# Scores from stacked high and low parts of q and k, in one-pass products, with q and k made two attentions ahead

## The chip, the core and the metric

The kernel runs on one core of a Trainium2 chip. The metric is the device time of one execution in microseconds (us), from the first to the last instruction. The profile shows one execution: each engine's instructions with start and duration, the waits between engines, and the packets of the DMA engines. TensorE does matrix products, VectorE (DVE in the profile) and ScalarE (ACT) elementwise work, GpSimd (POOL) elementwise work and some DMA issues, and SyncE (SP) only issues DMAs here. Each engine works through its own instructions in the order in which they were written.

## What is computed

Sixteen independent sequences of 256 tokens with 256 features pass through three attentions and an MLP. All data is fp32, with 16 heads of 16 features. The reference, cut down:

```python
q_norm = rmsnorm(query, g_q); c_norm = rmsnorm(context, g_c)          # layer 0
out = softmax(Q K^T * scale, masked keys) V  @ Wo
x = rmsnorm(query + out, g_out)
h = ln(x); q, k, v = h @ wq + bq, ...                                  # layer 1
x = x + attn(rope(q * scale), rope(k), v, causal=True) @ wo + bo
h = ln(x); q = h @ wq + bq; k, v = y @ wk + bk, y @ wv + bv            # layer 2
x = x + attn(rope(q * scale), rope(k), v, causal=False) @ wo + bo
x = x + gelu(ln(x) @ fc1 + b1) @ fc2 + b2
```

Layer 0 is a cross attention of x to the context y, layer 1 a causal self attention, layer 2 again a cross attention to y. So there are 48 attentions of 16 heads each.

## The kernel before

**Order of the work.** The 48 attentions run one after the other in an order written by hand (`ORDER`, one digit for each attention, the digit being its layer): layer 0 of several sequences first, then layers 1 and 2 mixed in, so that an attention's input is ready some attentions earlier. After them come the MLPs of pairs of sequences. All instructions are placed by hand under a manual schedule: the loop over `i` (line 1020) emits, for each block `n` of attention `i`, the scores of this block, the values of the block before, and then pieces of the work of attentions around it. What is emitted first on an engine is done first there, and a wait of one instruction holds up all that stand behind it on the same engine, SP's queue of DMAs included. I call the time from one attention's first scores to the next one's a slot.

**One attention.** Features lie on partitions in two chunks `t` of 128, that is 8 heads each; tokens lie on the free axis. `by_feature` (line 345) makes q and k this way, `by_token` (line 356) makes v and the output projection. In both, a product is split into four of 32 columns that write to different partitions and run side by side in the array.

**Scores.** A non-causal attention has four blocks, one for each pair of chunk `t` and key chunk `kc` (128 keys); a causal one has three. In `scores` (line 553) the array is cut the other way, in four groups of 32 rows. Each group holds two heads of 16 features, so the kernel masks q: `qm` holds q twice, once with the even heads zeroed and once with the odd ones (`parity`). One fp32 product of 32 rows of k with both masked q's, 512 columns, gives the scores of the two heads. The result goes to two PSUM tiles `S`, which ACT empties by the exponential into `pt`. `psS` has two buffers, so the next block's scores wait for both exponentials. In causal attentions GpSimd zeroes what lies above the diagonal (line 584). `values` (line 589) multiplies the exponentials with v, one product for each head, and keeps a column of ones in v for the sums.

**q and k.** `q` (line 481) and `k` (line 520) are emitted one attention ahead, in slot `i` for attention `i+1`. For layer 0, q is scaled by the row's root mean square and masked in two DVE instructions straight out of PSUM, and k is copied by ACT. For layers 1 and 2, `rotated` (line 463) adds the bias on ACT, then DVE shuffles a copy by half a head and multiplies both by cosine and sine tables; DVE adds them, and for q masks the sum twice (one mask sometimes on ACT, `second_mask`).

**After the values.** `take` (line 619) copies the values out of PSUM (ACT for the first chunk, DVE for the second, in `end`) and writes them to a DRAM tile `hop`; `end` then reads the sums back with one DMA and the heads with two (`oT`). `invert` (line 637) takes the reciprocals on DVE, writes them to `inv_hop` and reads them back broadcast (`inv`). `divide` multiplies, `project` applies the output weights and adds the residual, `finish` norms layer 0's result. All these DMAs stand in SP's queue.

**Turning.** The input of layers 1 and 2 has to be turned so that features lie on partitions. For most attentions DVE transposes blocks of 32 (`pieces_out`), SP writes them to a DRAM tile `turn_hop` and four DMAs bring them back (`pieces_in`), in a slot chosen by `turned_ahead`. The others are turned by TensorE (`turn`). For layer 0 the input is loaded already turned, and the factor for q goes through a small DRAM tile (`send`, two DMAs, and `receive`).

**Buffers.** Tiles of the pool `work` have two buffers unless said otherwise; PSUM has three banks for dense products (`psD`), two pairs for scores (`psS`) and one for values (`psA`).

## Time and profile before

| | us |
|---|---|
| median of 3 runs (927.35 to 927.95) | 927.66 |
| span of the profiled execution | 927.3 |
| from the first scores of attention 0 to those of attention 2 (10.1 to 41.9) | 31.8 |
| attentions 2 to 47, 46 slots (41.9 to 721.2) | 679.3 |
| MLP and rest (721.2 to the end) | 206.1 |
| TensorE busy | 913.6 |
| DVE busy | 689.0 |
| ACT busy | 531.0 |
| GpSimd busy | 348.7 |

A line of the profile that describes a group names the line of the kernel, the engine, the operation, the tiles written and read, shapes and count; then the busy time in us, the mean duration in ns, and the idle time of the engine just ahead of these instructions, with what ended it. An fp32 product appears as two records. Records of products that run side by side overlap, so their busy time is less than count times mean. Lines that describe the order of time begin with the start in us and the time that the piece took. A line marked SPq is a DMA issue: its time is that of issuing, and the transfer follows.

### The profile page before, as it was taken

The page shows a single profiled execution, that of the slowest core. Times are in us where ns is not written, and L with a number is a line of the kernel's source. Part 1 is how long each engine was busy: PE and PEld are TensorE (multiplying, and loading weights), DVE is VectorE, ACT ScalarE, POOL GpSimd, SP SyncE. Part 2 cuts the span into 40 slices and gives each one's busy share as a digit, 9 for nine tenths or more (in the row PEclk, how much of TensorE's full clock was granted, in tenths as well). Part 3 has the DMA queues.
Part 4 walks back from the last instruction along what each step waited for, and adds up shares of the span by engine and source line. Part 5 has one row for each costly group of instructions (what it writes and reads, how often), then busy time and mean ns, then how long its engine had stood idle before and what let it go on. Part 6 is the DMA issues. An engine that isn't in the chain of part 4 may idle for free.

```text
span 927.3 us, 29346 instructions
## 1 busy us (share of the span) xinstructions
PE 913.6 (99%) x12226; PEld 535.3 (58%) x12226; DVE 689.0 (74%) x1501; ACT 531.0 (57%) x744; POOL 348.7 (38%) x558
## 2 busy tenths in 40 slices
PE   8999999999999999999999999999999999999997
PEld 4444445445454555455445454455444799999997
DVE  4458678896879787968977778987877597777663
ACT  3666546665666665657656666666666633444440
POOL 4224655446363564633554432453233041111100
PEclk9999999999999999999999999999999999999999
DMA  9443554355243243442444433333222111122201
GB/s 292 159 116 108 156 151 146 123 153 145 87 144 115 92 151 107 133 126 83 136 138 131 128 107 104 92 98 108 85 82 67 54 38 47 55 69 69 70 24 48
DMA packets 112193, 100.52 MB, mean 108 GB/s; under 512 B 24299, under 2 KB 104051, under 8 KB 112051
## 3 DMA queue, kind: packets, MB, share of 16 engines
q1 hardware_dynamic: 106962, 83.59, 28.8%
q0 software_dynamic: 4400, 14.42, 5.3%
q8 instruction: 98, 1.61, 0.8%
q10 hardware_dynamic: 688, 0.54, 0.2%
q14 instruction: 45, 0.36, 0.1%
HBM read 59.70 MB, written 38.82 MB: 106 GB/s over the span
## 4 chain that ended last, share of the span: by engine, by line
PE 89%; DVE 6%; DMA 2%; issue 1%; SPq 1%; ACT 0%; POOL 0%; DVEq 0%
PE S L566 18%; PE A L605 17%; PE d L352 16%; PE d L364 15%; PE upX L788 6%; PE A L886 5%; PE downZ L886 3%; PE upZ L788 3%; PE d L886 2%; PE d L788 2%; DVE a L476 1%; DVE u L476 1%; PE d L286 1%; DVE u L472 1%; PE downX L886 1%
## 5 line engine op out<-in xcount | busy, mean ns | idle before, releaser
L577 ACT ACTIVATE pt<-S 128x1024 f32<-128x1024 f32 x224 | 217.3, 1022 | 134.0 <-PE S L566 133.9
L566 PE MATMUL S<-qm,kT 32*128 32x512 f32 (+1 forms) x1536 | 202.9, 601 | 4.7 <-DVE kT L525 4.5
L605 PE MATMUL A<-pt,va 128*32 128x256 f32 (+1 forms) x3072 | 189.6, 368 | 0.0
L605 PEld LDWEIGHTS A<-pt,va 128*32 128x32 f32 x3072 | 80.2, 109 | 154.3 <-issue 95.5
L577 ACT ACTIVATE pt<-S,sy 128x1024 f32<-128x1024 f32 x128 | 135.6, 1111 | 50.6 <-PE S L566 50.3
L584 POOL TENSOR_SCALAR_AFFINE_SELECT pt<-pt 128x512 f32<-128x512 f32 x128 | 86.3, 688 | 141.1 <-ACT pt L577 140.7
L566 PEld LDWEIGHTS S<-qm,kT 32*128 32x128 f32 x1536 | 62.4, 183 | 76.1 <-issue 42.1
L468 ACT ACTIVATE a<-d,qk_bias 128x256 f32<-128x256 f32 x128 | 53.7, 470 | 52.1 <-PE d L352 36.1
L340 POOL TENSOR_TENSOR cur<-cur,bias 128x512 f32<-128x512 f32 x48 | 69.7, 1458 | 31.6 <-DVE xn L271 31.3
L352 PE MATMUL d<-hT,sa 128*32 128x256 f32 x1024 | 61.1, 379 | 0.2 <-DMA hT<-turn_hop 0.2
L246 POOL TENSOR_SCALAR r_ln<-bmv 128x2 f32<-128x2 f32 x48 | 13.1, 272 | 125.8 <-DVE bmv L265 124.3
L476 DVE TENSOR_TENSOR u<-u,turn 128x512 f32<-128x512 f32 x64 | 57.3, 895 | 0.0
L810 ACT COPY g<-upX 128x512 f32<-128x512 f32 x28 | 15.0, 589 | 72.4 <-issue 67.5
L476 DVE TENSOR_TENSOR a<-a,turn 128x512 f32<-128x512 f32 x64 | 52.5, 821 | 2.2
L622 DVE COPY av<-A 128x512 f32<-128x512 f32 x47 | 32.0, 681 | 22.3 <-PE A L605 21.7
L472 DVE STREAM_SHUFFLE u<-a 128x512 f32<-128x512 f32 x64 | 47.4, 741 | 0.0
L826 ACT ACTIVATE g<-g,fb 128x256 f32<-128x256 f32 x96 | 41.0, 499 | 11.1 <-DVE g L815 11.1
L352 PEld LDWEIGHTS d<-hT,sa 128*32 128x32 f32 x1024 | 33.4, 110 | 22.2 <-issue 0.6
L656 DVE TENSOR_TENSOR oT<-oT,inv 128x512 f32<-128x512 f32 x48 | 38.3, 799 | 10.2 <-issue 6.3
L246 POOL TENSOR_SCALAR r_o<-ms_o 128x2 f32<-128x2 f32 x16 | 4.7, 293 | 105.7 <-DVE sq L254 98.5
L271 DVE TENSOR_SCALAR xn<-cur,bmv,r_ln 128x256 f32<-128x256 f32 x96 | 41.6, 483 | 0.8 <-POOL r_ln L247 0.8
L665 DVE TENSOR_TENSOR cur<-d,cur 128x512 f32<-128x512 f32 x32 | 21.6, 674 | 26.3 <-PE d L364 26.1
(158 smaller groups left out, 1612.5 us busy)
## 6 DMA issues: line engine op xcount, KB each, us to landing
hop<-av SPq DMA_DIRECT2D x96, 256.0 KB
oT<-hop SPq DMA_DIRECT2D x96, 128.0 KB
inv<-inv_hop SPq DMA_DIRECT2D x96, 128.0 KB
turn_hop<-turn SPq DMA_DIRECT2D x33, 256.0 KB
hT<-turn_hop SPq DMA_DIRECT2D x132, 64.0 KB
out<-res SPq DMA_DIRECT2D x15, 256.0 KB
cur<-in_x POOLq DMA_DIRECT2D x11, 256.0 KB, 3.4
y<-in_y POOLq DMA_DIRECT2D x11, 256.0 KB, 4.2
```

What stands on the lines that cost most here:

```text
L340: nc.gpsimd.tensor_tensor(t, t, bias_sb[:, row : row + D].unsqueeze(1).to_broadcast([P, NC, D]), ALU.add)
L352: nc.tensor.matmul(o, lhsT=w[:, k, at + t * P + j : at + t * P + j + 32], rhs=tokens, start=(k == 0), stop=(k == KC - 1), skip_group_check ...
L364: nc.tensor.matmul(ps[j : j + 32, c * D : (c + 1) * D], lhsT=some_tokens(src, k, c, j), rhs=w[:, k, at : at + D], start=(k == 0), stop=(k ...
L468: nc.scalar.activation(a[:, t], ps[:, t], AF.Identity, bias=bias[:, t : t + 1])
L472: nc.vector.stream_shuffle(u.rearrange("p t s -> p (t s)"), a.rearrange("p t s -> p (t s)"), SWAP)
L476: nc.vector.tensor_tensor(t, t, table.unsqueeze(1).to_broadcast([P, KC, S]), ALU.mult)
L566: nc.tensor.matmul(ps[:, j, 2 * m * u : 2 * m * (u + 1)] .rearrange("p (i s) -> p i s", i=2), lhsT=self.kT[r, t, kc * P : (kc + 1) * P], r ...
L577: nc.scalar.activation(pt[:, :, :w], ps[:, :, :w], AF.Exp, scale=scale)
L584: nc.gpsimd.affine_select(out=diag, in_=diag, compare_op=ALU.is_ge, fill=0.0, base=0, pattern=[[0, 2], [0, 2], [1, P]], channel_multiplier=-1,
L605: nc.tensor.matmul(self.av[32 * r : 32 * r + 32, i, q0:S], lhsT=self.va[:, kc, 8 * t + 2 * r + i, :], rhs=pts[r // 2][:, r % 2, i * m : (i ...
L788: nc.tensor.matmul(o if len(b.shape) == 2 else by_groups(o), lhsT=a[:, c * P : (c + 1) * P], rhs=b, start=(first and c % 2 == 0), stop=Tru ...
L886: nc.tensor.matmul(ps[:, c, :], lhsT=a[f // 2][:, f % 2, c * P : (c + 1) * P], rhs=b[:, f, :], start=(first and c == 0 and f == 0), stop=True,
```

## The change

Scores no longer use full fp32 products. Each rotated (or scaled) q and k is split into a high part, which ACT writes by a copy to the type float32r (`high`), and a low part, the difference to the full value, which DVE computes in place (`low`). Both lie in one tile `hl`. Two DMAs from 64 partitions each then spread q so that a head has 32 rows, its 16 features each twice in a row, the high and low part behind each other on the free axis (`q_out`, tile `qd`, 8 KB on each partition). Two DMAs spread k so that a head's 32 rows hold each feature's high part and low part in turn (`k_out`, tile `kd`, 4 KB). A product of a head's 32 rows of `kd` with `qd`'s high part, and a second with its low part added in PSUM, give all four combinations. Each is a float32r product of 256 columns (128 in the causal blocks of the second key chunk). Four heads run side by side in the four row groups, in two rounds, where before four products took two heads each. The masks go. Attention 0 keeps the old way.

The schedule is written anew: q's product is emitted in slot `i` for attention `i+2` in the last block but one, its bias and rotation in the last; k's product for `i+2` follows in the last block and its rotation in the first block of slot `i+1`, with the split and the DMAs in the first and second block there. `end`, `invert` and `project` are cut in parts (`sums_in`, `heads_in`, `inverses_in`, `o_mm`, `o_in`) that are emitted at other places. The two heads' halves are now heads 0 to 3 and 4 to 7 of a chunk, not even and odd ones, so the output weights keep their order. The weights of layer 0 and of the first MLP product share one tile `wide`: the latter are loaded from the last layer 0 attention on, and GpSimd's combining of MLP weights moves to later slots, into buffers of the pool. A fallback branch, not taken with these inputs, loads layer 0's weights again. Some MLP steps move one attention earlier. The core of the diff; of the methods for q and k and of the loop only what is new (the lines removed stand in the kernel above):

```diff
--- before
+++ after
...
+        def whole(self, which, bias_of):
+            self.parts_of[which] = hl = work.tile([P, 2, KC, S], F32, tag="hl", name="hl")
+            if self.layer > 0:
+                bias = qk_bias[:, 2 * (self.layer - 1) + bias_of, :]
+                for t in range(KC):
+                    nc.scalar.activation(
+                        hl[:, 1, t], self.ps[which][:, t], AF.Identity, bias=bias[:, t : t + 1]
+                    )
+        def shuffled(self, which):
+            if self.layer > 0:
+                a = self.parts_of[which][:, 1]
+                self.u = work.tile([P, KC, S], F32, tag="u", name="u", bufs=1)
+                nc.vector.stream_shuffle(
+                    self.u.rearrange("p t s -> p (t s)"), a.rearrange("p t s -> p (t s)"), SWAP
                 )
...
+        def rotated(self, which):
+            if self.layer > 0:
+                a, u = self.parts_of[which][:, 1], self.u
+                for t, table in ((a, cos_t), (u, sin_t)):
+                    nc.vector.tensor_tensor(
+                        t, t, table.unsqueeze(1).to_broadcast([P, KC, S]), ALU.mult
+                    )
+                nc.vector.tensor_tensor(a, a, u, ALU.add)
+        def high(self, which):
+            hl = self.parts_of[which]
+            src = self.ps[which] if self.layer == 0 and which == "k" else hl[:, 1]
+            nc.scalar.copy(hl[:, 0].bitcast(F32R), src)
+        def low(self, which):
+            hl = self.parts_of[which]
+            src = self.ps[which] if self.layer == 0 and which == "k" else hl[:, 1]
+            nc.vector.tensor_tensor(hl[:, 1], src, hl[:, 0], ALU.subtract)
+        def q_mm(self):
+            self.ps["q"] = by_feature(self.hT, self.w, 0)
+        def q_in(self):
+            self.whole("q", 0)
+        def q_turn(self):
+            if self.layer == 0:
                 nc.vector.tensor_tensor(
...
+                    self.parts_of["q"][:, 1], self.ps["q"],
+                    self.rq.unsqueeze(1).to_broadcast([P, KC, S]), ALU.mult,
                 )
...
+            else:
+                self.shuffled("q")
+                self.rotated("q")
+        def q_high(self):
+            self.high("q")
+        def q_low(self):
+            self.low("q")
+        def q_out(self):
+            self.qd = work.tile([P, 2, 2, KC, S], F32, tag="qd", name="qd")
+            for i in range(2):
+                src = self.parts_of["q"][64 * i : 64 * i + 64].rearrange("p h t s -> p (h t s)")
+                nc.sync.dma_start(
+                    out=self.qd[:, i].rearrange("p h t s -> p (h t s)"),
+                    in_=src.unsqueeze(1).to_broadcast([64, 2, 2 * KC * S]),
                 )
+        def k_mm(self):
+            self.ps["k"] = by_feature(self.kvT, self.w, D)
+        def k_in(self):
+            self.whole("k", 1)
+        def k_shuffle(self):
+            self.shuffled("k")
+        def k_turn(self):
+            self.rotated("k")
+        def k_high(self):
+            self.high("k")
+        def k_low(self):
+            self.low("k")
+        def k_out(self):
+            self.kd = work.tile([P, 2, KC, S], F32, tag="kd", name="kd")
+            for i in range(2):
+                nc.sync.dma_start(
+                    out=self.kd[:, i].rearrange("p t s -> p (t s)"),
+                    in_=self.parts_of["k"][64 * i : 64 * i + 64].rearrange("p h t s -> p h (t s)"),
+                )
...
             for u, (t, _) in enumerate(units):
-                for g, ps in enumerate(pss):
-                    for j in range(2):
-                        r = slice(32 * (2 * g + j), 32 * (2 * g + j) + 32)
+                if self.i == 0:
+                    for r, ps in rows:
                         nc.tensor.matmul(
-                            ps[:, j, 2 * m * u : 2 * m * (u + 1)]
-                            .rearrange("p (i s) -> p i s", i=2),
+                            ps[:, 2 * m * u : 2 * m * (u + 1)].rearrange("p (i s) -> p i s", i=2),
                             lhsT=self.kT[r, t, kc * P : (kc + 1) * P],
                             rhs=self.qm[r, t, :, q0:S], start=True, stop=True,
                         )
+                    continue
+                for i in range(2):
+                    at = m * (2 * u + i)
+                    for h in range(2):
+                        for r, ps in rows:
+                            nc.tensor.matmul(
+                                ps[:, at : at + m],
+                                lhsT=self.kd[r, i, t, kc * P : (kc + 1) * P].bitcast(F32R),
+                                rhs=self.qd[r, i, h, t, q0:S].bitcast(F32R),
+                                start=(h == 0), stop=(h == 1), skip_group_check=True,
+                            )
             pts = []
             for ps in pss:
                 pt = work.tile([P, 2, 512], F32, tag="pt", name="pt", bufs=PT_LIVE)
...
+                    at, half = (r, i) if self.i > 0 else divmod(4 * i + r, 2)
                     nc.tensor.matmul(
                         self.av[32 * r : 32 * r + 32, i, q0:S],
-                        lhsT=self.va[:, kc, 8 * t + 2 * r + i, :],
-                        rhs=pts[r // 2][:, r % 2, i * m : (i + 1) * m],
+                        lhsT=self.va[:, kc, 8 * t + 4 * i + r, :],
+                        rhs=pts[at // 2][:, at % 2, half * m : (half + 1) * m],
                         start=(first and i == 0), stop=final, skip_group_check=True,
                     )
             if final and t == 0:
...
         def end(self, copy=nc.vector.tensor_copy):
             self.take(1, copy)
+        def sums_in(self):
             heads = self.hop.rearrange("t i (r e) q -> (t i r) e q", e=32)
             nc.sync.dma_start(
                 out=self.sums[:, 0],
                 in_=heads[:, HD, :].rearrange("g (a b) -> g a b", b=2 * H),
             )
+        def heads_in(self):
+            heads = self.hop.rearrange("t i (r e) q -> (t i r) e q", e=32)
             for t in range(KC):
                 nc.sync.dma_start(out=self.oT[:, t], in_=heads[8 * t : 8 * t + 8, :HD])
+        def invert(self):
...
+        def inverses_in(self):
             self.inv = work.tile([P, KC, S], F32, tag="inv", name="inv")
             for t in range(KC):
                 nc.sync.dma_start(
-                    out=self.inv[:, t], in_=hop[t].unsqueeze(1).to_broadcast([8, HD, S])
+                    out=self.inv[:, t],
+                    in_=self.inv_hop[t].unsqueeze(1).to_broadcast([8, HD, S]),
                 )
...
+        def load_next(i, any_time=True):
+            if pieces:
+                nc.gpsimd.dma_start(out=pieces[0][0], in_=pieces[0][1])
+                del pieces[0]
+            elif any_time and i > 2 and due and due[0][0] <= i:
+                nc.gpsimd.dma_start(out=due[0][1], in_=due[0][2])
+                del due[0]
...
+            sent = turns.get(i)
+            final = len(a.blocks) - 1
+            next_one, next_two, third = (
+                j if j < N_ATT else None for j in (i + 1, i + 2, i + 3)
+            )
+            steady = i > 1
...
             for n in range(len(a.blocks)):
+                if n == 0:
+                    do(turns.get(i - 1), "pieces_in")
+                    if steady:
+                        do(next_one, "k_in")
+                if n == final and i > 0:
+                    do(next_two, "q_in")
                 a.scores(n)
                 if n > 0:
                     a.values(n - 1)
                 elif last is not None:
                     last.values(-1)
                 if n == 0:
+                    if steady:
+                        do(next_one, "k_shuffle")
+                    do(i - 1, "end")
+                    do(i - 2, "divide")
+                    if steady:
+                        do(next_one, "k_turn", "q_high", "q_low")
+                    if i > 0:
+                        do(next_two, "send")
+                    do(i - 1, "sums_in")
                     if i == 0:
+                        a.v_mm()
+                        a.v_in()
+                        do(1, "spread", "q_mm", "q_in")
+                        do(2, "stats")
+                    else:
+                        do(next_one, "v_mm")
+                    if i == 1:
+                        do(2, "q_mm", "q_in")
+                    if steady:
+                        do(next_one, "q_out")
...
+                if n == 1:
+                    if i > 0:
+                        do(next_one, "v_in")
+                    if steady:
+                        do(next_one, "k_high", "k_low")
+                    else:
+                        do(i + 1, "q_turn", "q_high", "q_low", "q_out", "k_mm", "k_in")
+                    do(i - 1, "invert")
+                    if steady:
+                        do(next_one, "k_out")
+                    if i > 0:
+                        do(next_two, "receive")
+                    do(i - 1, "inverses_in", "heads_in")
+                    if next_two is not None and next_two not in hosted and i > 0:
+                        do(next_two, "turn")
+                    do(i - 2, "o_mm", "o_in")
+                    for j in kept.get(i, ()):
+                        att(j).keep()
+                if n == final - 1:
+                    if not steady:
+                        do(i + 1, "k_high", "k_low", "k_out")
+                    if i == 0:
+                        do(2, "send", "receive", "turn")
+                        do(1, "v_mm", "v_in")
+                    do(i - 2, "finish")
+                    if i > 0:
+                        do(next_two, "q_mm")
+                    if sent is not None:
                         do(sent, "stats")
...
+                if n == final:
+                    if third is not None and third not in hosted:
+                        do(third, "stats")
+                    if sent is not None:
+                        do(sent, "pieces_out")
+                    if third is not None and third not in hosted:
+                        do(third, "norm")
+                    if i > 0:
+                        do(next_two, "q_turn", "k_mm")
...
```

## The prediction

> **What bounds the kernel now.** First the page, for who is busy and what the queues move:
>
> ```profile
> span 927.3 us, 29346 instructions
> PE 913.6 (99%) x12226; PEld 535.3 (58%) x12226; DVE 689.0 (74%) x1501; ACT 531.0 (57%) x744; POOL 348.7 (38%) x558
> q1 hardware_dynamic: 106962, 83.59, 28.8%
> ```
>
> TensorE never stops. SP's queue (q1) moved 83.59 MB in 28.8% of 16 engines' span: 83.59 / (0.288 x 927.3) = 313 GB/s while it moves. Then TensorE in order of time, inside one non-causal attention (a slot):
>
> ```profile
> 416.02 1.14 PE L566 MATMUL S<-qm,kT 32*128 32x512 f32 x8
> 417.10 1.07 PE L605 MATMUL A<-pt,va 128*32 128x256 f32 x16
> 417.98 1.91 PE L352 MATMUL d<-hT,sa 128*32 128x256 f32 x32
> 419.82 1.14 PE L566 MATMUL S<-qm,kT 32*128 32x512 f32 x8
> ```
>
> The starts matter: a scores block takes 1.07 us, the values 0.9 to 1.0, one dense product 1.84, and this repeats four times (three when causal) with nothing between. Within a scores block the trace has two sets of four concurrent records, 432 ns apart at 512 columns: 864 ns of streaming and about 0.2 us of change between the array's tilings. Next the stretches: slots 0 and 1, the 46 other attentions, and the MLP:
>
> ```profile
> core 0: us, PE busy (x) PEld busy (x) DVE busy (x) ACT busy (x) POOL busy (x), PEclk, DMA share, GB/s
> 10.10:26.60 16.50, 15.16 (x228) 7.08 (x224) 9.95 (x34) 9.32 (x12) 6.81 (x17) 1.00 1.07 358
> 26.60:41.90 15.30, 15.30 (x208) 6.84 (x208) 5.79 (x20) 10.05 (x11) 3.12 (x8) 1.00 0.38 117
> 41.90:721.20 679.30, 674.69 (x10304) 332.10 (x10300) 532.84 (x1138) 429.70 (x542) 307.72 (x484) 1.00 0.39 118
> 721.20:927.30 206.10, 201.08 (x1414) 185.75 (x1410) 136.63 (x297) 79.93 (x178) 27.88 (x37) 1.00 0.16 51
> ```
>
> The 46 slots take 679.3 / 46 = 14.8 us each, with DVE busy 11.6 and ACT 9.3 of it. Last, SP's issues around one slot's start (scores at 399.1 and 411.8):
>
> ```profile
> 402.02 0.37 SPq L623 DMA_DIRECT2D hop<-av  x1
> 404.27 0.54 SPq L630 DMA_DIRECT2D sums<-hop  x1
> 404.87 1.21 SPq L635 DMA_DIRECT2D oT<-hop  x2
> 406.18 2.92 SPq L317 DMA_DIRECT2D hT<-turn_hop  x4
> 409.15 0.43 SPq L644 DMA_DIRECT2D inv_hop<-sums  x1
> 410.88 1.21 SPq L650 DMA_DIRECT2D inv<-inv_hop  x2
> ```
>
> SP is one file of waits. hop<-av (256 KB) to the issue that waits for its landing is 2.25 us; inv_hop to inv (16 KB) 1.73 us, almost all fixed. Today nothing that TensorE needs soon stands in this file: q and k go from DVE to scores directly.
>
> [...] The kernel before has no large transfer from 64 partitions, so its trace is silent. [...] the same 128x512 add costs 692 ns into kT and 1116 ns on average in q, where GpSimd is working:
>
> ```profile
> L492 DVE TENSOR_TENSOR a<-a,u 128x512 f32<-128x512 f32 x32 | 35.7, 1116 | 1.1
> L525 DVE TENSOR_TENSOR kT<-a,u 128x512 f32<-128x512 f32 x32 | 22.2, 692 | 1.1
> ```
>
> **The change, part by part.**
>
> *TensorE, removed.* Per unit and eight heads, two sets of 432 ns become four sets (two halves, q high and q low) of 256 columns [...]. 864 becomes 436: 0.43 us saved. 31 non-causal attentions x 4 x 0.43 = 53 us; 16 causal x 2 x 0.43 = 14 us; the causal units of 128 columns gain about nothing[...]. Attention 0 keeps the old path. Sum 67 us. TensorE's own work per slot falls to about 13.4 us (non-causal) and 11.9 (causal). Bounds: no gain if a set takes 216 ns; a loss of 149 us if the four row groups take turns (432 ns a set: 156 units of 256 columns at +0.86, 32 of 128 at +0.43).
>
> *DVE and ACT.* For layers 1 and 2 both masks go (487 + 480 ns) and two subtractions of 690 come; for layer 0 two products of 742 become three of about 690. DVE +0.4 us per slot, to 12.0. ACT gains two copies of about 590 ns for layers 1 and 2 and one for layer 0: +1.0, to 10.3. Both lie under TensorE's 13.4 by sum, but the q high copy now waits in ACT's file for a rotation on DVE, with the next exps behind it, and DVE's subtraction waits for that copy.
>
> *DMA, added.* Per attention q_out moves 2 x 512 KB and k_out 2 x 256 KB, SBUF to SBUF, 1.57 MB where a slot moved about 1.75 (118 GB/s x 14.8). Each reads 64 partitions. [...] at the page's 313, 3.35 and 1.7. [...] Four more issues of about 0.45 us on SP.
>
> *The new chain.* In slot i, from its first scores to those of i+1, which need both tiles:
>
> - scores 0.64 and the last attention's values 1.0, drained: 1.85
> - DVE's copy of av 0.65 (row L622, 681 less overlap): 2.5
> - hop issue to landing 2.25: 4.75; sums issue 0.54, ahead of q_out: 5.3
> - q_out issue 0.45 and start 0.5: 6.2; 4.8 of data: 11.0
> - k_out right behind, 2.4: 13.4; landing and semaphore 0.6: 14.0
>
> An undisturbed slot thus takes 14.0, over the 13.4 and 11.9 of TensorE. Three things lengthen it. pieces_in now stands first in the slot: its four issues (some 0.44 each) and the wait for turn_hop are ahead of hop in 23 slots, about 1.9 us: 0.95 per slot. send's two rq_hop issues (0.53 each) precede sums for 14 slots: 0.3. DVE comes late to q_low[...]: (821 - 691) + (895 - 684) + (1116 - 692) = 0.76 us in one rotation by the group means, taken as 0.85 with the waits on ACT. Sum 16.1 us per slot. Also q_in(i+2) needs the buffer that q_out(i+1) is still reading: it stalls on ACT in front of the last block's exps, so TensorE cannot run ahead.
>
> *Slot 0 and 1.* Start-up loads hold the DMA engines until about 27 us (share 1.07, 358 GB/s to 26.6), ahead of q_out(1) and k_out(1): 27 + 4.8 + 2.4 + 0.6 = 34.8 instead of 26.6. With slot 1 at 16: start of slot 2 at 51 instead of 41.9.
>
> *Edits at nothing.* Weight loads shared in one wide tile, later fc1 and combining on GpSimd (POOL 38% busy), w0's reload only in the branch not taken, Wo's row order, MLP steps one slot earlier (same TensorE work). GpSimd's slack covers them; without it each combine step is 1.7 us.
>
> Sum: 51 + 46 x 16.1 (741) + 206 + 7 for late exps and first-time waits = 1005 us, against the profile's own 927.3; the median 927.66 is the same within 0.04%, so no correction.
>
> **Rivals.**
>
> *Hidden after all (faster).* Place: k_out's landing before scores(i+1). [...] the chain is 6.2 + 3.35 + 1.7 + 0.6 = 11.85, under TensorE's slot; it decides once k_out lands before 13.4 (non-causal) and 11.9. Then 927.3 - 67 + 8 (start) = 868. For: DMA share only 0.39 over those slots. Against: 11.85 leaves nothing for the 2.1 us of delays in causal slots.
>
> *In-order files eat the gain.* DMA at full rate, but ACT and DVE wait for each other (q_turn, high, low) and for hl's buffer, with exps behind: slots about 14.9 on average, as now: 47 + 46 x 14.9 + 206 = 938, from 905 to 965. For: DVE at 12.0 of 13.4, often 15 in non-causal slots now. Against: slack of two attentions.
>
> *No concurrency or no single pass.* Sets of 432 ns: 927.3 + 149 = 1076 before any wait. Against: fp32 row groups do run together today.
>
> **How the numbers follow.** Chain 0.50 (950 to 1045), in-order files 0.20, hidden 0.22, no concurrency 0.08. Prediction: the chain's 1005. The range 870 to 1050 leaves out half of the hidden case and nearly all of the last, under 0.2. Within 0.2% is what a measurement of this kernel can't tell from none. Faster: 0.22 and 0.06 of the in-order case, 0.28; same 0.02; slower 0.70.
>
> **What would show it.** Right: TensorE waiting at slot starts for DMA kd, some 2 us per slot, PE near 80% busy; q_out packets of 4 KB slower than the 159 ns of today's 4 KB loads; ACT idle before its bias copies on hl. Scores sets 109 ns apart show the saving; 216 or 432 refute it. Wrong: q_out's 1 MB moving in under 3.5 us, or kd never awaited; then the result falls to the first two rivals.

## The result, and the profile after

The changed kernel takes 1216.41 us (median; 1209.40 to 1222.51) against 927.81 us of the kernel before: ratio 1.311, interval 1.306 to 1.316. The forecast was 1005, with a range to 1050: the direction was right, and the loss is 289 us where 77 were expected.

First the page of the kernel after, for the same three lines as before and the granted clock in 40 slices:

```profile
span 1213.7 us, 32814 instructions
...
PE 965.4 (80%) x13730; PEld 623.3 (51%) x13730; DVE 708.4 (58%) x1521; ACT 559.9 (46%) x818; POOL 338.1 (28%) x558
...
PEclk9889788878898888897988788888889889999999
...
q1 hardware_dynamic: 134034, 157.53, 47.2%
```

TensorE is busy 80% of the span, as the chain case said. But its busy time is longer than before (965 against 914 us), although its work is less. The clock row says why: through all the attentions the granted clock is 0.7 to 0.9. Next the stretches of start, 46 slots and MLP:

```profile
core 0: us, PE busy (x) PEld busy (x) DVE busy (x) ACT busy (x) POOL busy (x), PEclk, DMA share, GB/s
0.00:62.20 62.20, 41.90 (x612) 20.86 (x613) 21.98 (x71) 23.03 (x28) 15.99 (x43) 0.89 0.75 222
62.20:1009.30 947.10, 724.18 (x11717) 418.32 (x11717) 549.79 (x1153) 457.92 (x614) 294.27 (x478) 0.86 0.58 159
1009.30:1213.70 204.40, 199.37 (x1402) 184.17 (x1402) 136.59 (x297) 78.91 (x176) 27.87 (x37) 1.00 0.16 52
```

A slot takes 947.1 / 46 = 20.6 us instead of 14.8. The start is 20 us longer, the MLP 2 us shorter. In the 46 slots TensorE now idles 223 us (before: 5). In the trace's record of the clock, 197 us of its busy time there fall into stretches granted half the speed (before: 3). If that work took half the time at full speed, the clock costs about 98 us of busy time (an estimate from these numbers). What is left, 724 - 98 = 626 us, stands against 673 before (675 less half of the 3): the score products do save, about 47 us by this reckoning. Idle +218, clock +97, work -47 make the 268 us of the slots; the start adds 20.

TensorE inside one slot, by time (to be held against the four lines of the kernel before):

```profile
463.20 1.91 PE L352 MATMUL d<-hT,sa 128*32 128x256 f32 x32
471.36 0.58 PE L633 MATMUL S<-qd,kd 32*128 32x256 f32 x2 [6.25 <-ACT pt L644]
472.27 1.22 PE L633 MATMUL S<-qd,kd 32*128 32x256 f32 x14 [0.33 <-ACT pt L644]
473.42 2.49 PE L673 MATMUL A<-pt,va 128*32 128x128 f32 x32
475.73 1.90 PE L364 MATMUL d<-sa,hT 128*32 128x256 f32 x32
477.56 0.74 PE L633 MATMUL S<-qd,kd 32*128 32x256 f32 x16
478.24 1.07 PE L673 MATMUL A<-pt,va 128*32 128x256 f32 x16
```

At 477.56 a block of scores at full clock: values follow after 0.68 us where they followed after 1.08. From 471 to 475, behind 6.25 us of waiting, the same kinds of product take far longer. Of a block cut in two by a further wait, the last 14 records take 1.22 us, where all 16 take 0.74 at full clock. The 32 records of values (16 of 128 columns and 16 of 256, which the view merges) take 2.49 us; in the kernel before such a group took 1.51:

```profile
412.86 1.51 PE L605 MATMUL A<-pt,va 128*32 128x128 f32 x32
```

The clock of these stretches in the kernel after:

```profile
466.00:470.00 4.00, 0.00 (x0) 0.00 (x0) 0.78 (x4) 0.45 (x2) 0.00 (x0) 0.83 0.95 221
470.00:474.00 4.00, 2.31 (x28) 1.76 (x32) 3.45 (x5) 4.00 (x8) 2.54 (x3) 0.50 0.59 202
...
478.00:482.00 4.00, 4.00 (x84) 2.37 (x80) 3.16 (x6) 2.64 (x4) 0.00 (x0) 1.00 0.10 33
```

SP's issues in the same slot:

```profile
453.43 0.47 SPq L311 DMA_DIRECT2D turn_hop<-turn  x1
457.27 1.76 SPq L317 DMA_DIRECT2D hT<-turn_hop  x4
459.13 0.38 SPq L691 DMA_DIRECT2D hop<-av  x1
461.97 0.55 SPq L700 DMA_DIRECT2D sums<-hop  x1
462.62 1.22 SPq L532 DMA_DIRECT2D qd<-hl  x2
464.56 1.32 SPq L717 DMA_DIRECT2D inv_hop<-sums  x1
465.96 2.65 SPq L560 DMA_DIRECT2D kd<-hl  x2
469.63 1.29 SPq L724 DMA_DIRECT2D inv<-inv_hop  x2
```

The slot's first scores are at 452.2. SP waits from 453.9 to 457.3 for turn_hop with hop behind it, then issues hop only at 459.1 and q_out at 462.6. The issue of inv_hop, 0.34 us in the kernel before, takes 1.3 us behind q_out's bulk, and so does each of the two of k_out.

ACT in the same slot:

```profile
469.55 0.84 ACT L471 ACTIVATE hl<-d,qk_bias 128x256 f32<-128x256 f32 x2 [9.39 <-DMA qd<-hl]
470.28 1.94 ACT L644 ACTIVATE pt<-S 128x1024 f32<-128x1024 f32 x2
```

Last the waits of all engines over the slots (total us, times, longest):

```profile
POOL pt L651 <- ACT pt L644: 269.5, 82, 11.0
ACT pt L644 <- PE S L633: 232.4, 102, 11.4
ACT hl L471 <- DMA qd<-hl: 225.4, 31, 11.4
PEld S L633 <- ACT pt L644: 187.8, 87, 8.1
...
PE S L633 <- ACT pt L644: 146.2, 56, 7.6
...
PE S L633 <- DMA kd<-hl: 49.9, 20, 5.4
```

and those of SP's queue:

```profile
SPq L691 <- DVE av L690: 104.7, 23, 9.4
SPq L317 <- DMA turn_hop<-turn: 92.4, 23, 5.2
SPq L700 <- DMA hop<-av: 78.1, 38, 3.9
SPq L724 <- DMA inv_hop<-sums: 53.0, 45, 2.9
```

The forecast looked for TensorE waiting for kd. That wait exists, but has only 50 us. The largest wait for a DMA is ACT's: q's bias copy waits for q_out of the attention before, which still reads hl, and TensorE waits for the exponentials behind it. (The two longer waits in the list are for exponentials and scores, which come late themselves.) This was the first theory to test.

### The profile page after: what moved, and what is told of

Same layout as the page of the kernel before. It is cut to its first block, busy times and chain, and to the rows that moved or that the text cites. A ratio compares the mean times of both kernels' runs of the same rounds, so it can differ in the third digit from the quotient of the medians.

```text
span 1213.7 us, 32814 instructions
## 1 busy us (share of the span) xinstructions
PE 965.4 (80%) x13730; PEld 623.3 (51%) x13730; DVE 708.4 (58%) x1521; ACT 559.9 (46%) x818; POOL 338.1 (28%) x558
## 4 chain that ended last, share of the span: by engine, by line
PE 46%; DMA 29%; DVE 8%; ACT 6%; issue 5%; SPq 4%; POOL 2%; ACTq 0%; DVEq 0%
DMA qd<-hl 16%; PE d L364 10%; PE A L673 10%; PE S L633 7%; DMA kd<-hl 6%; PE upX L893 5%; ACT pt L644 4%; PE A L991 4%; PE d L352 3%; PE downZ L991 2%; PE upZ L893 2%; DMA turn_hop<-turn 2%; DMA hop<-av 2%; ACT hl L471 2%; PE d L991 1%
## 5 line engine op out<-in xcount | busy, mean ns | idle before, releaser
L633 PE MATMUL S<-qd,kd 32*128 32x256 f32 (+1 forms) x3008 | 169.0, 328 | 211.7 <-ACT pt L644 146.2
L633 PEld LDWEIGHTS S<-qd,kd 32*128 32x128 f32 x3008 | 121.8, 205 | 297.0 <-ACT pt L644 188.6
L673 PE MATMUL A<-pt,va 128*32 128x256 f32 (+1 forms) x3072 | 226.9, 426 | 5.1 <-DVE av L690 4.6
L471 ACT ACTIVATE hl<-d,qk_bias 128x256 f32<-128x256 f32 x128 | 54.5, 485 | 233.1 <-DMA qd<-hl 225.4
L502 DVE TENSOR_TENSOR hl<-hl 128x512 f32<-128x512 f32 x79 | 56.9, 720 | 14.8 <-ACT hl L496 14.8
L496 ACT CAST hl<-hl 128x512 fp32r<-128x512 f32 x79 | 48.9, 619 | 24.1 <-DVE hl L490 24.1
L490 DVE TENSOR_TENSOR hl<-hl,u 128x512 f32<-128x512 f32 x64 | 50.4, 788 | 2.2
L715 DVE RECIPROCAL sums<-sums 128x32 f32<-128x32 f32 x48 | 16.9, 352 | 58.9 <-DMA sums<-hop 58.3
L487 DVE TENSOR_TENSOR hl<-hl,turn 128x512 f32<-128x512 f32 x64 | 47.3, 739 | 1.1
L479 DVE STREAM_SHUFFLE u<-hl 128x512 f32<-128x512 f32 x64 | 46.9, 732 | 0.2
```

The source lines that it names most:

```text
L471: nc.scalar.activation(hl[:, 1, t], self.ps[which][:, t], AF.Identity, bias=bias[:, t : t + 1])
L487: nc.vector.tensor_tensor(t, t, table.unsqueeze(1).to_broadcast([P, KC, S]), ALU.mult)
L502: nc.vector.tensor_tensor(hl[:, 1], src, hl[:, 0], ALU.subtract)
L633: nc.tensor.matmul(ps[:, at : at + m], lhsT=self.kd[r, i, t, kc * P : (kc + 1) * P].bitcast(F32R), rhs=self.qd[r, i, h, t, q0:S].bitcast(F ...
L673: nc.tensor.matmul(self.av[32 * r : 32 * r + 32, i, q0:S], lhsT=self.va[:, kc, 8 * t + 4 * i + r, :], rhs=pts[at // 2][:, at % 2, half * m ...
```

## The experiments

### One wait at a time

Theory A: ACT's wait for hl's buffer is the missing term. Theory B: the transfers set the slot and this wait mirrors them. Four edits (shortened here), each alone:

```diff
 # third hl buffer
-hl = work.tile([P, 2, KC, S], F32, tag="hl", name="hl")
+hl = work.tile([P, 2, KC, S], F32, tag="hl", name="hl", bufs=3)   # inv and a: bufs=1
 # exponentials first
-if n == final and i > 0: do(next_two, "q_in")
 a.scores(n)
+if n == final and i > 0: do(next_two, "q_in")
 # all partitions
-out=self.qd[:, i], in_=self.parts_of["q"][64 * i : 64 * i + 64] (each row twice)
+out=self.qd[:, i], in_=self.parts_of["q"]
-out=self.kd[:, i], in_=self.parts_of["k"][64 * i : 64 * i + 64] (p h)
+out=self.kd[:, i], in_=self.parts_of["k"][:, i]
 # q_out first
 do(i - 1, "end")
+do(next_one, "q_high", "q_low", "q_out"); do(i - 1, "sums_in")
 do(i - 2, "divide"); do(next_one, "k_turn"); do(next_two, "send")
```

> The changed kernel with three buffers for hl instead of two (room from one buffer each for inv and a). q's bias copy on ACT then no longer waits for the transfer q_out of the attention before. Theory A, the missing term of the forecast: the slot is a loop that goes from q_out's landing through the waiting bias copy and the exponentials behind it to the next scores; with the wait gone the slot falls from 20.6 us to the forecast chain of 16 to 18 us, and the time to 1040 to 1100 us; the wait for qd ahead of the bias copy (225 us) falls under 20 us and the wait of the scores for kd rises from 50 to over 100 us. Theory B, the DMA transfers themselves set the slot and the wait on ACT only mirrors them: the wait moves to kd in full and the time stays above 1180 us.

> The changed kernel with q's bias copy emitted behind the last block's scores, so behind its exponentials on ACT; still two buffers for hl. Theory A (what hurts is that exponentials stand behind the wait): the exponentials, and with them the values, the copy of av and hop, come some 3 to 5 us earlier in the slot, and the time is 1040 to 1110 us, about as with a third buffer, though ACT still waits for qd. Theory A' (what hurts is that q itself is made late): no gain, above 1190 us. Theory B (the transfers set the slot): above 1180 us.

> The changed kernel with the same bytes, packets and DMA issues for q_out and k_out, but each reads all 128 partitions of hl instead of 64 (what arrives in qd and kd is then not what the scores need: the scores are of wrong rows, the work is the same). If reading 64 partitions halves the rate, as the forecast took it, the 4 KB packets fall from 307 to about 160 ns, q_out's 1 MB from 4.9 to 2.5 us, and with q_out in the loop of every slot the time falls by 46 x 2.4 = 110 us to about 1105 (1080 to 1140). If the packets are slow for another reason (SBUF to SBUF, or two writes for each row), they stay near 300 ns and the time above 1195.

> The changed kernel with q_low on DVE ahead of divide and of k's rotation, and q_out on SP ahead of send and sums_in; nothing else. Theory A: q_out is issued at about 5 us of the slot instead of 11, because it waits neither for k's rotation on DVE nor for hop's landing on SP; the loop through the bias copy shortens by 4 to 6 us, until k_out, which comes about 1 us later, sets the slot at 16.5 to 18: 1020 to 1090 us. Theory B (DMA work of about 13 us per slot sets the slot, whatever the order): above 1150 us.

Measured: third buffer 1198.88 us (1197.99 to 1202.69), exponentials first 1209.50, q_out first 1211.64, all partitions 1120.37 (1117.98 to 1123.42). The edits meant to shorten ACT's wait gain 5 to 18 us, not the 100 and more that theory A asked for: it falls. The waits over the slots with the third buffer show where the time went:

```profile
ACT pt L644 <- PE S L633: 300.4, 124, 11.6
PE S L633 <- DMA kd<-hl: 174.3, 55, 8.1
...
ACT hl L471 <- DMA qd<-hl: 86.6, 23, 6.8
```

ACT's wait for qd falls from 225 to 87 us, and the scores' wait for kd rises from 50 to 174: one wait took the other's place, and the slot stayed at 20.3 us. The third buffer took one each from inv and a, but exponentials first, which leaves all buffers as they are, shows the same exchange (93 and 172 us). With q_out first, q_out is issued at 8.7 us of the slot instead of 11.4 (medians) and its packets end at 14.9 instead of 18.0. But k_out is issued at 16.7 instead of 14.9: in SP's file it stands behind inv_hop, and the reciprocals that inv_hop needs start 5.4 us after the issue of sums instead of 2.2, some 0.9 us after q_out's last packet. In the changed kernel and in these three k_out's packets end 20.2 to 20.6 us after the slot's first scores. These edits moved waits about ahead of that end, and it stayed.

Reading all 128 partitions gains 96 us, within the range expected; k_out's packets then end at 17.6 us. Median time of a 4 KB packet on SP's queue fell from 307 to 160 ns, and that of k_out's 2 KB packets, which never read a row twice, from 121 to 85; k_out's issue on SP from 1360 to 618 ns, and inv_hop's from 1439 to 344. k_out's line in the kernel after and in this one (shortest, median and longest issue in ns):

```profile
L560 SPq DMA_DIRECT2D kd<-hl x94: 524/1360/2961, 26.6 to 982.1; - x94
```

```profile
L559 SPq DMA_DIRECT2D kd<-hl x94: 464/618/1478, 26.8 to 887.0; - x94
```

The three edits that leave the results as they are, together:

> The changed kernel with the three edits that alone gave 0.3 to 1.4 per cent, together: three buffers for hl, the last block's exponentials ahead of q's bias copy, and q_low and q_out ahead of k's rotation and of sums_in. Theory E: each slot has several loops of nearly equal length (q's through ACT and DVE, k's through the scores, SP's file), and all hold the two transfers; loosened together the first shortens, and the time falls to 1140 to 1180 us. If the transfers and what queues behind them set the slot alone, the three together give no more than the best one alone (1199): above 1190.

1219.81 us (1215.35 to 1223.26): nothing. They do not add: k_out is issued later still (17.2 us), and its packets end at 20.9. Theory E, several loops loosened together, found no support in these three edits; none of them brings k_out's end forward.

### SP's file and its queue

Next theory, C: SP's file of issues and landings sets the slot.

```diff
 # pieces later: pieces_in behind k_out in block 1, not first in the slot
 # ACT's queue: q_out behind k_high in block 1, k_out in block 2
-nc.sync.dma_start(...)      # q_out, k_out
+nc.scalar.dma_start(...)
 # both queues: the same places, half i of each on
+(nc.sync, nc.scalar)[i].dma_start(...)
```

> The changed kernel with pieces_in (the wait for turn_hop and four issues on SP) emitted behind k_out in the second block instead of first in the slot, ahead of hop. New theory C: SP's file of issues and landings sets the slot, not a single wait of ACT or TensorE; in 23 slots SP waits 92 us in all for turn_hop (4.0 us each) with hop, sums and q_out behind it. Then the time falls by 60 to 90 us, to 1125 to 1155. If the slot is set by the two transfers alone (7.2 us of data) and by what follows them, SP's order hardly matters: above 1195.

> The changed kernel with q_out's and k_out's four DMAs issued on ACT's queue (q_out behind the copy for k's high part in the second block, k_out in the third block) instead of SP's; same bytes, same 64 partitions. Theory C (SP's file): SP loses 182 us of issues, the 40 us by which inv_hop's issue is slowed, and the landings of inv_hop and hop no longer queue behind 1.57 MB; the slot falls to about 16 us, which is the transfers' own chain, and the time to 970 to 1040. Theory D (the half-rate transfers themselves, in whatever queue, are what each slot waits for): the 4 KB packets still take 307 ns, and the time stays above 1150.

> As the kernel with ACT's queue, but the half of q_out and k_out that reads partitions 0 to 63 is issued on SP and the other half (64 to 127) on ACT's queue, at the same places. If 64 partitions at a time are the limit, the two halves now run side by side, the packets are faster when both run, and this is faster than the version with all on ACT's queue by up to 46 x 2 us; if SP's file is what matters, it is slower than that version by the two issues of about 0.6 us and their waits, 20 to 60 us.

> The changed kernel with three things together: three buffers for hl, pieces_in later, and the two halves of q_out and k_out on SP's and ACT's queues. Theory C: each removes time from SP's file or a wait that follows from it, so the gains add where they did not singly: 930 to 1000 us. If a third hl buffer is worth nothing even now, it is within 10 us of what the two others give.

1247.12, 1264.93 (1263.36 to 1274.67), 1376.51 and 1412.29 us: all are slower than the changed kernel, and theory C's times were missed by 90 us and more. The first two lie in the open ranges written for its rivals (above 1195 and above 1150), but no text foresaw that they would lose against the changed kernel. The traces show why the edits did not test the theory cleanly. With pieces later, hT's loads stand behind k_out's bulk, and the dense product for q waits for them: 112 us in 11 waits. On ACT's queue SP is rid of four issues, but the small transfers on SP's queue land later; SP's waits over the slots:

```profile
SPq L717 <- DVE sums L715: 156.1, 46, 6.6
SPq L724 <- DMA inv_hop<-sums: 130.0, 46, 6.2
SPq L700 <- DMA hop<-av: 121.8, 36, 7.0
```

The wait for inv_hop's 16 KB rose from 53 to 130 us and for hop from 78 to 122, with the 4 KB packets still at 308 ns. At these later places of q_out and k_out, a second queue did not take the small transfers out of the bulk's way. But q_out and k_out also come later in this kernel, and the two effects were not separated. With both queues k_out is in the third block too, where SP's half stands behind the landing of inv_hop. SP in that kernel:

```profile
468.32 1.31 SPq L724 DMA_DIRECT2D inv<-inv_hop  x2
...
471.42 0.58 SPq L560 DMA_DIRECT2D kd<-hl  x1
```

SP's half of k_out goes out at 471.4, ACT's half went at 463.5, and the scores wait for kd 390 us in all the slots. q_out's halves do not run side by side in this slot either: ACT's packets end at 462.9, SP's begin at 463.4. So these two runs say nothing on whether two halves side by side are faster; the 112 us over ACT's queue alone fit SP's late half, but nothing else was held fixed to show it.

### How much are the bytes?

```diff
 # small transfers: 512 bytes of each row
-out=qd[:, i] (p, h t s)
+out=qd[:, i] (p, h t s)[:, :128]        # k_out: the same
-lhsT=self.kd[r, i, t, kc * P : (kc + 1) * P], rhs=self.qd[r, i, h, t, q0:S]
+lhsT=self.kd[r, i, 0, 0:P], rhs=self.qd[r, i, 0, 0, 0:P], broadcast to m columns
 # bytes unawaited: as small transfers, and behind k_out, for both halves
+nc.sync.dma_start(out=spare_q, in_=w.unsqueeze(1).to_broadcast([64, 2, 1024]))
+nc.sync.dma_start(out=spare_k, in_=w.rearrange("p (h n) -> p h n", h=2))
```

> The changed kernel with q_out and k_out cut to their first 128 columns (512 bytes from each partition: 0.26 MB per attention instead of 1.57), same issues, waits and order; the scores read these columns again and again (so they are not the reference's scores; TensorE's work is the same). If the two transfers make the loss (theory E), the slots fall from 20.6 to 14.5 to 15.5 us and the time to 930 to 975 us, with TensorE's clock back near 1. If the order of work itself, with its splits and in-order files, makes it, the time stays above 1080.

> The version with small transfers of q and k, and right behind k's the bytes that were cut as four more transfers on the same queue, read from 64 partitions of a weight and written to DRAM tiles that nobody reads: full traffic (and a little more), but neither q nor k waits for its own bulk. If the loss comes from q and k arriving late, this is within 60 us of the version with small transfers alone. If it comes from the bulk standing in the one queue ahead of the sums, inverses and pieces, it stays above 1120.

> The version whose transfers read all 128 partitions (1120 us, wrong rows for the scores, same work), with the three edits (third hl buffer, exponentials first, q_out first). Theory E: the loops without the half rate are shorter by 2 us already; loosened they fall to 16 to 17.5 us a slot, 1000 to 1065 us. If nothing but the bytes matters, within 10 us of 1120.

Small transfers: 1071.19 us (1067.22 to 1075.74). So five sixths of the bytes (1.31 of 1.57 MB) are worth 145 us, half of the loss, and the other half stays without them: both of the outcomes written down were too simple. Bytes unawaited: 1343.43 us, slower than the changed kernel itself. The scores wait for kd only 13 us there; but inv's issue on SP takes 1.24 us instead of 0.62, divide waits for oT 226 us in 44 waits, and q's bias copy waits 96 us for the next small q_out, as the bulk stands ahead of all three. (This kernel also has four more issues on SP and writes to DRAM; how much of the 272 us is theirs was not measured.) So bulk that no reader waits for does harm through what stands behind it in the queue; how much of the 145 us comes that way, this run does not say. All partitions with the three edits: 1109.09 us (1105.75 to 1116.47), 11 less than all partitions alone, and no sign of the 1000 to 1065 of theory E; rate and edits hardly add.

### The other half: order

Before, pieces_in stood behind hop; now it stands first in the slot.

```diff
-do(turns.get(i - 1), "pieces_in")       # first in block 0
 ...
 do(i - 1, "end")
+do(turns.get(i - 1), "pieces_in")       # behind hop, ahead of sums_in
```

> Small transfers (first 128 columns of q and k only, scores of these columns; 1071 us), and pieces_in emitted behind hop again, as in the kernel before, instead of first in the slot. SP waits 80 us for turn_hop in the small-transfer kernel, in 23 slots, with hop behind it. If this order is what remains of the loss: 1071 - 60 to 90 = 980 to 1010 us. If not: above 1050.

> The changed kernel at full bytes with only pieces_in moved behind hop, ahead of sums_in. If SP's order adds to the transfers: 1216 - 50 to 90 = 1125 to 1165 us. If other loops of the same length take over, as for the other single edits: 1190 to 1216.

> Small transfers, pieces_in behind hop, a third hl buffer and the last block's exponentials ahead of q's bias copy. In the small-transfer kernel q's bias copy still waits 77 us for q_out and 65 us for DVE, with exponentials behind. If these waits and SP's order are the remainder, they go: 930 to 975 us. If the remainder is DVE's and ACT's work itself: within 15 us of the version without the third buffer.

> Transfers that read all 128 partitions (wrong rows for the scores, same work; 1120 us alone), with pieces_in behind hop, the third hl buffer and the exponentials first. If rate and order add: 1000 to 1050 us. If the full-rate bytes still set the slot in the one queue: 1090 to 1120.

With small transfers 1028.55 us (1025.76 to 1030.93): 43 less. At full bytes 1178.16 us (1170.90 to 1178.44): 38 less. Both fall between the two outcomes written down: the order on SP is a cause of its own and adds to the bytes, but a smaller one than expected. At full bytes hop is issued at 4.6 us of the slot instead of 7.4 (medians), but sums only at 9.3 instead of 10.3, as pieces_in now stands between the two. All partitions with pieces back and two edits: 1072.11 us, 48 less than all partitions alone, again between its two outcomes. But small transfers, pieces back, a third hl buffer and exponentials first took 1056.85, 28 more than without the last two, which neither outcome allowed for; why is open (the third buffer again takes one each from inv and a). SP's waits with small transfers, first without pieces back:

```profile
SPq L694 <- DVE av L693: 101.7, 26, 8.2
SPq L703 <- DMA hop<-av: 89.7, 38, 4.2
SPq L317 <- DMA turn_hop<-turn: 79.9, 23, 4.8
```

and with it:

```profile
SPq L694 <- DVE av L693: 144.3, 44, 8.3
SPq L703 <- DMA hop<-av: 41.1, 20, 4.6
...
SPq L317 <- DMA turn_hop<-turn: 28.2, 16, 4.0
```

turn_hop fell from 80 to 28 us and the wait for hop's landing from 90 to 41, but hop's own wait for DVE's copy of the values rose from 102 to 144: part of the gain moved there. DVE does rotations and norms ahead of this copy. So the copy went to ACT:

```diff
-def end(self, copy=nc.vector.tensor_copy):
+def end(self, copy=nc.scalar.copy):
```

> Small transfers (first 128 columns, scores of these columns), pieces_in behind hop (1029 us), and the copy of the last values out of PSUM on ACT instead of DVE. If hop's wait for DVE's file is the remainder, SP's 133 us of waiting for this copy shrinks under 50 and the time falls by 50 to 90 us, to 940 to 980. If the remainder is the length of DVE's own work between its waits (splits, rotations, finishing), it stays above 1010.

> The changed kernel at full bytes with pieces_in behind hop (1178 us) and the copy of the last values on ACT. If hop's place counts beside the transfers: 1178 - 40 to 80 = 1100 to 1140 us. If ACT, which here still waits for q_out with q's bias copy, is as late as DVE: 1165 to 1190.

1015.87 us (1015.47 to 1016.62) and 1163.21 us (1160.39 to 1171.36): 13 and 15 less, a small gain, twice the same, where 50 to 90 and 40 to 80 were forecast if hop's wait for DVE were the remainder. The copy is late on ACT as well (98 us). 1163 is the fastest version found that computes the scores as they should be; none of the kernels beats the one before.

What the chain of runs accounts for, of 289 us: 145 most of the bytes of the two transfers (1216 to 1071), 43 the place of pieces_in (to 1029), 13 the place of the copy of the values (to 1016). The last 88 us are not settled. They can be placed, though: the start is 11 us later than before, and the slots take 757 us instead of 679. There TensorE idles 94 us (89 more than before) and has 77 us of busy time at half clock (about 37 more), less 48 of work saved. The idle time stands behind waits spread over DVE, ACT and SP, none of which was shown to be the one.

## Why the prediction was wrong

**TensorE's saving.** Right in kind: four row groups run together, and their sets of 256 float32r columns start 117 ns apart, where sets of 256 fp32 columns start 216 ns apart in the kernel before; a block of scores takes 0.68 us instead of 1.08. The size, 67 us, came out as about 47. An undisturbed block saves 0.40 us where 0.43 were forecast with sets 109 ns apart, the author's estimate: no run had shown a float32r set yet. That would make 60 us in the 46 slots; the rest is unexplained (blocks cut in two by a wait are one candidate). The prediction also misread the sets before: those of 512 columns start 533 ns apart in an undisturbed block, not 432 (twice the 216). The sum hardly moves, because about 0.2 us of a block were counted apart, as change of tilings; the kernel before does show more time there (the first set of scores starts 329 ns after the last dense one of 256 columns, where dense sets start 216 apart), but what the 101 ns more between two sets of scores are was not shown. As forecast, the causal blocks of 128 columns gain next to nothing (1.05 us instead of 1.08): their sets start 112 ns apart.

**The half rate.** Right. 307 ns for a 4 KB packet from 64 partitions makes 256 x 307 / 16 = 4.9 us for q_out. The 4.8 forecast, and the 2.4 for k_out, were the author's estimates: no trace of the kernel before showed the rate of such a transfer. With the same bytes read from all 128 partitions the packet took 160 ns; what makes it slow from 64 was not shown.

**The chain of a slot: the step that failed, by its terms.** Forecast 16.1 us, measured 20.6; 46 times the difference is 207 of the 209 us between the forecast and the profiled 1213.7 (a start 11 us later than forecast, less the allowance of 7 and 2 of the MLP, makes up the rest). Medians of the times in a slot:

| | forecast | measured |
|---|---|---|
| last issue of hop | 4.3 (2.5, with 0.95 for pieces_in and 0.85 for DVE) | 7.4 |
| hop's issue to the issue of sums | 2.25 (of one slot; the median before is 2.5) | 3.0 |
| q_out's first issue to the end of its packets | 0.9 + 4.8 | 6.4 (issue at 11.4) |
| end of k_out's packets | 13.4 + 2.1 of delays | 20.2 (issue 14.9 + 5.3) |

The path fits the one forecast: k_out's packets end 0.4 us before the slot does (0.6 forecast), q_out's first packet starts 1.2 us after its first issue does (0.95 forecast; both forecasts were estimates), and of the edits at full bytes those that brought their end forward (all partitions to 17.6 us, pieces back to 19.3) gained most. The terms were too small, by 4.7 us at that end. The largest is hop's lateness, 3.1 us. In the 23 slots with pieces_in DVE's copy starts at 3.45 us on average, and hop is issued at 8.29: 4.1 us after the copy's end, where 1.9 were priced. The four issues were counted, and hardly more than 0.1 us left for turn_hop's landing. But SP reaches turn_hop's own issue only 1.7 us into the slot, since inverses_in ahead of it waits for inv_hop's landing: inv is issued 5.4 us after inv_hop (1.7 before) and 0.9 us after q_out's last packet (medians). So SP waits out turn_hop's whole flight, 4.6 us from its issue. In the other 23 slots DVE's copy itself starts only at 5.2: the rotation and a norm that waits 2.0 us for GpSimd's factor now stand ahead of it. The other terms carry the second error: the durations of hop, inv_hop and the issues were taken from the kernel before, whose DMA engines were idle 61% of these slots (share 0.39). With 1.57 MB more in the same file hop's 256 KB, inv_hop's 16 KB and even the issues behind q_out take longer.

**The wait on hl.** The prediction named it, "it stalls on ACT in front of the last block's exps", and gave it no price. It is the largest wait for a DMA in the profile after (225 us), yet an edit that takes 139 us of it away gains 18 us. Leaving it unpriced cost the forecast little; believing the view of waits would have cost more.

**The clock.** No step spoke of it. The two traces record only the clocks 1.0 and 0.5. In the slot shown the half speed lasts for 4 us of work after a wait of 6.3 us, but shorter waits stood ahead of it too: of the 40 stretches at half speed that begin in the slots, 10 had no wait as long as 3.4 us (the shortest of these stretches) in the 3.4 us ahead of them; in one the longest was 1.84 us. The one stretch in the slots of the kernel before followed a wait of 1.92 us. So even the "some 2 us per slot" that the prediction expected for kd could have cost clock. All waits were priced in idle time alone; the products behind them ran at half clock, about 98 us of busy time. How much of that lies on the path was not tried.

**The rivals as alternatives.** "In-order files eat the gain" was priced at 938 with the transfers at full rate. The run with small transfers is a kinder test of it, and gives 1071. It was no rival to the chain: 145 us go with the bytes and 143 stay without them in the same kernel, while the chances treated the two as one or the other. Of the 143, order is shown for 43 and the place of the copy for 13. Adding the two cases at their own prices (78 and 11 us) would have given about 1016, so both prices were too low as well. The "hidden" case failed at its own condition, k_out landing before 13.4 us; "no concurrency" is refuted by the sets of 117 ns.

**What would show it.** TensorE near 80% busy, slow q_out packets, sets close to 109 ns and ACT idle before its bias copies all came; "TensorE waiting at slot starts for DMA kd" came with about half the size (50 us over 46 slots, 1.1 each), while the wait for exponentials took 146.

## What to carry to other kernels

A transfer added to a queue that carries short dependent hops has to be charged to every hop behind it, not only to its own reader (here the median issue of inv_hop went from 0.34 to 1.44 us): redo the hops' durations at the new load, and add the costs of order and of bytes instead of choosing between them. When several chains end at the same place, a long wait in the profile is no measure of what its removal gains (139 us of waiting less, 18 us of gain). Ask instead which event the slot's end follows, here the end of k_out's packets, and whether an edit brings it forward. And idle time on TensorE costs more than itself where the granted clock falls behind it: here about 98 us beside 223 of idling.

## What the runs showed of the hardware

- After 6 us without a product (465.1 to 471.4) the granted clock was 0.50 until 475.5: sets of scores started 213 ns apart there, and 117 ns at 477.8. In the 46 slots of the changed kernel such stretches covered 197 us of busy time; before, where the longest wait was 1.92 us, they covered 3.
- In the 46 slots of these two traces the half speed lasts 3.4, 6.8 or 10.2 us at a time. When the time at full speed is cut backwards, from each fall, into stretches of 3.41 us, TensorE was busy at most 51% of the last stretch ahead of each of the 40 falls in the changed kernel, and at least 41% of the 161 others; before, 44% ahead of the one fall and at least 64% of the 196 others.
- The issues of inv_hop on SP took longer where much of q_out was still to be moved on the same queue. In the changed kernel 39 of 47 issues of inv_hop came with 220 or more of q_out's 256 packets unfinished; the median of all was 1439 ns. With all 128 partitions read 35 of 45 came with fewer left and took about 344 ns, and with q_out on ACT's queue the median on SP was 338.
- Moving the bulk to a second queue (and to later places) made the small transfers of the first slower, not faster: SP's wait for inv_hop rose from 53 to 130 us.
